# Layer 1's quotients in 32x32 blocks, the ends of its halves behind all its scores, and another order of VectorE's work in the last chunk

## The chip, the cores and the metric

The kernel runs on one core of one Trainium2 chip. The metric is the device time of one execution in microseconds (us), as a median of several runs. A profiled execution gives a trace of every instruction on the engines: TensorE (PE; its weight loads are PEld), VectorE (DVE), ScalarE (ACT), GpSimd (POOL) and SyncE (SP, which here only issues DMAs). Lines such as L1163 are lines of the kernel's file.

## What is computed

Four self-attention layers, one after the other, on x of shape (4, 64, 64, 64): four samples of 4096 positions with 64 channels. The layers differ in the normalisation ahead of them and in the residual; what matters here is layer 1, a SAGAN block whose keys and values are max-pooled to 1024 positions:

```python
theta = x @ w_theta            # 4096 positions x 8
phi   = maxpool2(x @ w_phi)    # 1024 positions x 8
g     = maxpool2(x @ w_g)      # 1024 positions x 32
beta  = softmax(theta @ phi^T) # 4096 x 1024, rows sum to one
out   = x + sigma * ((beta @ g) @ w_o + b_o)
```

(w_theta, w_phi, w_g, w_o are spectrally normalised first.) The other three layers are attention over 4096 x 4096 positions with 64 channels. In all of them the kernel forms exp(scores) without a maximum, multiplies it with the values, and divides by the row sums afterwards: that quotient is what the change is about.

## The kernel before, in words

**The foreground.** `fast_path` (L598) takes the samples s0 to s3 through the layers. Layers 0, 2 and 3 run as attention phases of 64 calls of `step()` (L813) each; with three phases for each of four samples that makes 768 steps. A step issues, in this order: scores for two units (L1290 in layers 2 and 3, L997 in layer 0), 16 matmul records of 512 columns; their exponentials on ScalarE (L1295, L1007), 128x1024 each, from a PSUM score tile into an SBUF tile; then the two accumulations that fall due in this step (exp(scores) times values into PSUM, L1325 or L1028, 16 records). In layers 2 and 3 VectorE adds each exponential tile to a running sum `zacc` (L1301), in pairs. At the end of each chunk of 512 positions, `turn_blocks` and `sum_blocks` transpose zacc in blocks of 32x32 (L1309) and reduce it over 32 (L1313), `sums` (L1239) adds up the partial sums with four small matmuls (L1244, 16 columns each) and takes the reciprocal of 128x16 sums on VectorE (L1249, L1252), and `turn` (L1259) transposes the output's 32x32 blocks (L1264), multiplies by the reciprocals (L1257, L1271) and goes on.

**The background.** Everything else is cut into pieces by `yield` in generators; `background(tempo, ...)` (L779) sets the generator that runs next to a phase, and each step advances it at most once at each of four places: MID (between the step's two accumulations), LATE (inside the second one), END, and ALONE (as MID, but then nothing is done LATE in the same step). The budget is a credit that grows by `tempo` with each step. Work that has a due time of its own goes into the lists `urgent`, `before`, `due` and `later`; `urgent` takes the MID place ahead of the background. The order on every engine is the order in which the program issues (L623, `manual_schedule`); each engine works its queue in that order.

**Buffers.** PSUM holds two score tiles of 128x1024 (`s_tile`, pool of 2) and four accumulators of 128x512 (`acc_tile`, pool of 4). A score tile can only be written again when its reader has finished: ScalarE's exponential, as a rule, or VectorE where a piece has borrowed the tile. SBUF has 13 tiles of `x_tile` and 14 of `p_tile`; `small` and `o_tile` have two of each name.

**Layer 1** (L1063) is background work. For s0 it runs beside layer 0 of s1 (`on` "DVE", `bank` False); for s1, s2 and s3 beside layer 2 of the sample before (`on` "ACT", `bank` True). After its projections (L1076, L1093, L1105) come two halves j of 2048 positions, each with 8 blocks of keys k: `scores(j, k)` (L1121, operands of 8 rows), their exponentials on ScalarE (L1127), their sum on VectorE (`zaccs[j]`, L1136), and `add(j, k)` (L1147) with values of 32 columns, into one accumulator (bank) or into a score tile that VectorE adds up (not bank, L1156); at the end ScalarE moves the accumulator to SBUF (L1158).

Then `finish(j)` for each half: `normalise(j)` and `last(j)`. `normalise` multiplies a matrix of ones with `zaccs[j]`, four calls over 512 columns (L1163), which puts the sums of a position into all 32 rows of its quarter; ScalarE copies that to SBUF and records a sum for the range check (L1169); VectorE takes the reciprocal in four parts of 128x128 (L1172) and multiplies the half's output with it (L1174); ScalarE reads the reciprocals once more for the check (L1176). `last` multiplies with w_o (L1182) and VectorE adds bias and residual (L1184). With `bank`, `finish(0)` begins as soon as half 0 is complete, a piece of it after each block of half 1 (L1212 to L1222), and `finish(1)` follows half 1. Without `bank`, both begin behind all scores and run side by side.

**The last chunk.** In layer 3 of s3, the last chunk's `final` (L1548) replaces `turn`: it works in two parts of 256 columns. `count_bad` (L1826) reduces the range checks to one number by way of a small matmul (L1829), `set_bad` writes it out (L1830), and `read_flag` makes every engine load it before the last stores (L1540): whether a general path runs depends on that number; it does not run here. `most_in_range` (L1813) has checked all earlier sums some steps before.

Of the kernel before, what the change touches and what calls it, by code (L numbers as in the profile page):

```python
# [8 lines left out]
FP = mybir.dt.float32  # L9
I32 = mybir.dt.int32  # L10
AF = mybir.ActivationFunctionType
ALU = mybir.AluOpType
AX = mybir.AxisListType
# [584 lines left out]
def fast_path(tc: tile.TileContext, a: dict, out: bass.AP, bad, read_flag):  # L598
# [9 lines left out]
    nc = tc.nc  # L608
    x = a["x"]
    B, H, W, C = x.shape  # L610
    N = H * W
    P = 128
    W2 = W // 2
    S = N // 2
    NC = S // 512
    NB = N // P
# [3 lines left out]
    MID, ALONE, LATE, END = range(4)  # L620
# [4 lines left out]
    const, small = pool("const", 1), pool("small", 2)  # L625
# [3 lines left out]
    s_tile = lambda: ps_s.tile([P, 1024], FP, tag="s", name="s")  # L629
    acc_tile = lambda: ps_a.tile([P, 512], FP, tag="a", name="acc")  # L630
    x_tile = lambda name: x_p.tile([P, S], FP, tag="x", name=name)
    p_tile = lambda: p_p.tile([P, 1024], FP, tag="p", name="p")
    o_tile = lambda name: o_p.tile([P, 512], FP, tag=name, name=name)
    half = lambda i: slice(i * C, (i + 1) * C)
    quarter = lambda q: slice(q * 32, q * 32 + 32)
    chunk = lambda c: ds(c * 512, 512)
# [18 lines left out]
    def ctile(shape, name):  # L655
        return const.tile(shape, FP, tag=name, name=name)
# [53 lines left out]
    ident = ctile([P, P], "ident")  # L710
    make_identity(nc, ident)
    ones = ctile([P, P], "ones")
    nc.gpsimd.memset(ones, 1.0)
    lanes = ctile([P, C], "lanes")
    nc.vector.tensor_reduce(lanes[:, 0:32], ident.rearrange("p (a j) -> p j a", j=32), AX.X, ALU.add)
    nc.vector.tensor_copy(lanes[:, 32:C], lanes[:, 0:32])

    def twice(dst, src):
        for i in range(2):
# [22 lines left out]
    blocks = {n: (ctile([P, P], f"A{n}"), ctile([P, 1], f"Ab{n}")) for n in (0, 3)}  # L742
# [3 lines left out]
    rows(gamma0, a["L0_conv_gamma"])  # L746


    NCHECK = B * (NB + 2 + 2 * NC * 16)
    all_z, all_r = ctile([P, NCHECK], "all_z"), ctile([P, NCHECK], "all_r")  # L750
    checks = [0]

    def check_columns(n):
        i = checks[0]
        checks[0] += n
        return all_z[:, i : i + n], all_r[:, i : i + n]
# [306 lines left out]
    def layer1(on, st, bank):  # L1063
# [7 lines left out]
        s = s_tile()  # L1071
        for j in range(2):
            for e in range(2):
                for i in range(2):
                    q = 2 * e + (i ^ j)
                    nc.tensor.matmul(  # L1076
                        s[quarter(q), chunk(i)], wth1[half(i), quarter(q)], x1[half(i), chunk(2 * j + e)],
                        start=True, stop=True,
# [3 lines left out]
        NK = M // P  # L1082
# [5 lines left out]
        for j in range(NC // 2):  # L1088
            yield MID
            s = s_tile()  # L1090
# [12 lines left out]
        s = s_tile()  # L1103
# [7 lines left out]
        ps, accs, zaccs, os = {}, {}, {}, {}  # L1111
# [46 lines left out]
                nc.scalar.copy(os[j], acc)  # L1158

        def normalise(j):  # L1160
            z = acc_tile() if bank else s_tile()[:, 0:512]
            for q in range(4):
                nc.tensor.matmul(  # L1163
                    z[quarter(q), :], ones[:, 0:32], zaccs[j][:, q // 2, chunk(q % 2)], start=True, stop=True
                )
            del zaccs[j]
            r = o_tile("r")
            z_column, r_column = check_columns(1)
            nc.scalar.activation(r, z, AF.Copy, accum_out=z_column)  # L1169
            for i in range(4):  # L1170
                yield MID
                nc.vector.reciprocal(r[:, ds(i * P, P)], r[:, ds(i * P, P)])  # L1172
            yield MID
            nc.vector.tensor_tensor(os[j], os[j], r, ALU.mult)  # L1174
            yield MID
            nc.scalar.activation(r, r, AF.Copy, accum_out=r_column)  # L1176

        def last(j):
            s = s_tile()
# [4 lines left out]
            nc.vector.scalar_tensor_tensor(x1[:, wide(j)], s, bo1, x1[:, wide(j)], ALU.add, ALU.add)  # L1184

        def finish(j):

            if not bank:
                yield ALONE
            yield from normalise(j)  # L1190
            yield MID
            yield ALONE
            last(j)

        end = None
        todo = [(j, k) for j in range(2) for k in range(NK)]
        for n in range(len(todo) + 1):
            accumulate = None
            if n < len(todo):
                yield LATE  # L1200
                accumulate = scores(*todo[n])
            if n:
                if not bank:
                    yield END
                elif n == len(todo):
                    yield LATE
                add(*todo[n - 1])
            if accumulate and bank:
                later.append(accumulate)
            elif accumulate:  # L1210
                accumulate()
            if n == NK and bank:  # L1212
                end = finish(0)
                at = next(end)
            elif end is not None:
                yield at
                at = next(end, None)
                end = end if at is not None else None
        while end is not None:
            yield at  # L1220
            at = next(end, None)
            end = end if at is not None else None  # L1222
        if bank:
            yield from finish(1)
        else:
            ends = [finish(j) for j in range(2)]
            at = [next(end) for end in ends]
            while at[0] is not None:
                if at[0] == ALONE:
                    yield ALONE  # L1230
                    at[0] = next(ends[0], None)
                yield at[1]
                at = [at[0] if at[0] != at[1] else next(ends[0], None), next(ends[1], None)]
# [5 lines left out]
    def sums(zsums):  # L1239

        s = s_tile()
        for k in range(2):
            for i in range(2):
                nc.tensor.matmul(  # L1244
                    s[half(i), ds(k * 512, 16)], lanes[half(k), :], zsums[half(k), i * 16 : i * 16 + 16],
                    start=True, stop=True,
                )
        z_columns, r_columns = check_columns(16)
        nc.vector.tensor_reduce(  # L1249
            z_columns, s.rearrange("p (k b) -> p b k", k=2)[:, 0:16, :], AX.X, ALU.add  # L1250
        )
        nc.vector.reciprocal(r_columns, z_columns)  # L1252
        return z_columns, r_columns
# [270 lines left out]
    def layer3(st, not_before):  # L1524


        h = st.pop("x"), st["k"][1]
        dst = out[st["b"]].rearrange("(j e b) (i w) (q f) -> j e b i w q f", e=2, b=16, i=2, q=2)

        def residual(c):  # L1530

            t = o_tile("residual")
            for e in range(2):
                nc.vector.transpose(t[half(e), :], h[0 if e == c % 2 else 1][half(e), chunk(c // 2 * 2 + e)])
            return t

        def store(c, t, rows, queues):
            for n in range(4):
                e, q = divmod(n, 2)
                queues[n % len(queues)](  # L1540
                    dst[c // 2, e, rows, c % 2, :, q, :].rearrange("b w f -> w b f"), blocked(t[quarter(n), :])[:, rows, :]
                )

        def last(c, t):
            nc.vector.tensor_tensor(t, t, residual(c), ALU.add)
            store(c, t, slice(0, 16), [nc.sync.dma_start])

        def final(acc, zsums):  # L1548

            z_columns, r_columns = sums(zsums)  # L1550
            rest_in_range(z_columns, r_columns)
            t = o_tile("turned")
            parts = [slice(m * 256, m * 256 + 256) for m in range(2)]
            for m, cols in enumerate(parts):
                o = o_tile("o")[:, 0:256]
                nc.scalar.copy(o, acc[0][:, cols])
                nc.vector.tensor_tensor(o, o, acc[1][:, cols], ALU.add)
                nc.vector.transpose(t[:, cols], o)
                if m == 0:
                    set_bad = count_bad()  # L1560
            for m, cols in enumerate(parts):
                divide(blocked(t[:, cols]), t[:, cols], r_columns[:, m * 8 : m * 8 + 8])
                if m == 0:
                    set_bad()
                nc.vector.tensor_tensor(t[:, cols], t[:, cols], kept[0][:, cols], ALU.add)
            flag.append(read_flag())
            for m in range(2):
                store(NC - 1, t, slice(m * 8, m * 8 + 8), [nc.sync.dma_start, nc.scalar.dma_start])

        kept = []  # L1570
        ends = st["b"] == B - 1
        if ends:
            before.setdefault(now[0] + NC * NB // 2 - 8, []).append(lambda: later.append(lambda: kept.append(residual(NC - 1))))
        return attention(st, last, not_before, "done3", final if ends else None)
# [14 lines left out]
    t = s_tile()[:, 0:P]  # L1589
# [5 lines left out]
    t = s_tile()[:, 0:1]  # L1595
# [65 lines left out]
    at = 10 * C  # L1661
    loaded = {}
    for n, dsts in spectra:
        w_d, u_d = a["L1_conv_w_" + n], a["L1_conv_u_" + n]
        r, d = w_d.shape
# [147 lines left out]
    def most_in_range():  # L1813
        assert checks[0] == NCHECK - count
        for i, (seen, bound) in enumerate(((all_z, SUM_MAX), (all_r, 1.0 / SUM_MIN))):
            seen = seen[:, 0 : NCHECK - count]
            nc.vector.tensor_scalar(seen, seen, bound, None, ALU.is_le)
# [71 lines left out]
```

## Time and profile before

| what | value |
|---|---|
| three runs, median (lowest to highest) | 2941.55 us (2941.31 to 2942.19) |
| the profiled execution, its own time | 2942.68 us |
| its span on the trace, from first to last instruction | 2940.5 us |
| granted TensorE clock, mean | 0.999 of full speed |
| busy: ScalarE, VectorE, GpSimd | 65%, 63%, 1% |
| a plain step (16 score and 16 accumulation records) | 3.43 us |
| the same with the score and value matmuls of one block of layer 1 (bank) | 5.64 us |

A step's length is read off the trace as the distance between the first score matmuls of one step and of the next. "Span" is what the trace covers; the profiled execution's own time is 2.2 us longer. In the lists of groups a line gives the operation, output and input, partitions x columns, the number of instructions, their busy time and the mean of one in nanoseconds; then the idle time of the engine ahead of them and what ended it. The chain of waits follows the work back from the last instruction, each time to what released it.

### The profile page before, as it was taken

What the parts mean: (1) busy time and instruction counts of PE and PEld (TensorE: products, weight loads), DVE (VectorE), ACT (ScalarE), POOL (GpSimd) and SP (SyncE); (2) the same over time, 40 slices, a digit from 0 to 9 for tenths busy, and PEclk for the clock granted to TensorE, in tenths of its full rate; (3) what the DMA queues carried; (4) which work ended last, traced back from release to release, by engine and by line L of the source; (5) the groups of instructions that cost most, each with busy time, mean ns of one, the idle gap of its engine ahead of it and who ended that gap; (6) DMA issues with size and microseconds to landing.
All of it is one profiled execution on the core that took longest, in us unless ns stands there. A gap on an engine that the chain in (4) does not pass through costs nothing.

```text
span 2940.5 us, 66599 instructions
## 1 busy us (share of the span) xinstructions
PE 2910.9 (99%) x29349; PEld 1169.8 (40%) x29349; DVE 1846.6 (63%) x2112; ACT 1923.4 (65%) x2769; POOL 33.6 (1%) x32
## 2 busy tenths in 40 slices
PE   9999999999999999999999999999999999999998
PEld 3333235333544433444443334444344444443332
DVE  1211742588831068872017888888988877878877
ACT  6877778666588866567886665655655555655554
POOL 0000000000000000000000000000000000000000
PEclk9999999999999999999999999999999999999999
DMA  2010000000002000000000000000000100000000
GB/s 38 1 30 5 1 2 7 13 5 12 13 5 30 1 5 5 19 6 13 6 1 5 5 21 7 20 5 9 5 19 5 23 5 7 6 19 5 8 5 10
DMA packets 76778, 30.12 MB, mean 10 GB/s; under 512 B 70464, under 2 KB 74560, under 8 KB 75072
## 3 DMA queue, kind: packets, MB, share of 16 engines
q1 hardware_dynamic: 74224, 25.37, 4.6%
q8 instruction: 232, 3.80, 0.5%
q10 hardware_dynamic: 2256, 0.41, 0.1%
q14 instruction: 66, 0.54, 0.1%
HBM read 4.79 MB, written 4.19 MB: 3 GB/s over the span
## 4 chain that ended last, share of the span: by engine, by line
PE 97%; DVE 1%; ACT 1%; SPq 0%; issue 0%; DMA 0%; ACTq 0%; DVEq 0%
PE acc L1325 30%; PE s L1290 30%; PE acc L1028 15%; PE s L997 15%; PE s L1121 2%; PE acc L1147 2%; ACT p L1127 1%; PE s L1147 1%; DVE zacc L1301 0%; PE s L888 0%; PE s L909 0%; PE s L1421 0%; PE s L1093 0%; PE s L1182 0%; PE s L1469 0%
## 5 line engine op out<-in xcount | busy, mean ns | idle before, releaser
L1295 ACT ACTIVATE p<-s 128x1024 f32<-128x1024 f32 x1024 | 993.7, 1022 | 687.7 <-PE s L1290 654.9
L1301 DVE TENSOR_TENSOR zacc<-zacc,p 128x1024 f32<-128x1024 f32 x960 | 1173.2, 1222 | 182.6 <-ACT p L1295 119.3
L1325 PE MATMUL acc<-p,v 64*64 64x512 f32 (+1 forms) x8576 | 1019.9, 572 | 0.0
L1325 PEld LDWEIGHTS acc<-p,v 64*64 64x64 f32 x8576 | 356.4, 133 | 532.9 <-issue 529.2
L1028 PE MATMUL acc<-p,vs 64*64 64x512 f32 (+1 forms) x4224 | 513.5, 578 | 0.5 <-ACT vs L1017 0.5
L1007 ACT ACTIVATE p<-s 128x1024 f32<-128x1024 f32 x480 | 486.9, 1015 | 32.9 <-PE s L997 14.0
L1290 PE MATMUL s<-q,k 64*64 64x512 f32 x2048 | 498.0, 590 | 1.7 <-ACT p L1127 1.7
L997 PE MATMUL s<-xT,q 64*64 64x512 f32 x2048 | 488.8, 591 | 2.6 <-DVE mean L1357 0.7
L1290 PE MATMUL s<-q,xT 64*64 64x512 f32 x2048 | 490.2, 589 | 0.0
L997 PE MATMUL s<-xT,q_swapped 64*64 64x512 f32 x2048 | 489.1, 591 | 0.7 <-DVE o L1156 0.7
L1290 PE MATMUL s<-q,h_swapped 64*64 64x512 f32 x2048 | 479.3, 589 | 0.2 <-DVE v L1446 0.2
L1290 PE MATMUL s<-q,k_swapped 64*64 64x512 f32 x2048 | 476.2, 590 | 0.0
L1009 DVE TENSOR_REDUCE all_z<-z 128x1 f32<-128x4 f32 x128 | 20.1, 157 | 624.4 <-ACT p L1007 624.1
L1028 PEld LDWEIGHTS acc<-p,vs 64*64 64x64 f32 x4224 | 186.7, 133 | 262.4 <-issue 199.0
L1017 ACT ACTIVATE vs<-v,all_r 64x64 f32<-64x64 f32 x512 | 176.7, 345 | 139.5 <-PE acc L1028 70.8
L997 PEld LDWEIGHTS s<-xT,q_swapped 64*64 64x64 f32 x2048 | 149.7, 133 | 143.3 <-issue 108.8
L1290 PEld LDWEIGHTS s<-q,h_swapped 64*64 64x64 f32 x2048 | 150.1, 133 | 135.4 <-issue 127.5
L1290 PEld LDWEIGHTS s<-q,xT 64*64 64x64 f32 x2048 | 150.5, 133 | 133.2 <-issue 127.4
L1290 PEld LDWEIGHTS s<-q,k_swapped 64*64 64x64 f32 x2048 | 149.9, 133 | 132.8 <-issue 88.3
L997 PEld LDWEIGHTS s<-xT,q 64*64 64x64 f32 x2048 | 149.3, 133 | 127.4 <-issue 96.7
L1290 PEld LDWEIGHTS s<-q,k 64*64 64x64 f32 x2048 | 150.2, 133 | 112.7 <-issue 94.2
L1127 ACT ACTIVATE p<-s 128x1024 f32<-128x1024 f32 x128 | 124.1, 1021 | 80.7 <-PE s L1121 80.7
(218 smaller groups left out, 1320.8 us busy)
## 6 DMA issues: line engine op xcount, KB each, us to landing
k_swapped<-k SPq DMA_DIRECT2D x8, 512.0 KB, 5.4
residual<-turned SPq DMA_DIRECT2D x128, 32.0 KB, 1.8
h_swapped<-xT SPq DMA_DIRECT2D x8, 512.0 KB, 5.8
out_dram<-turned SPq DMA_DIRECT2D x60, 64.0 KB, 2.0
xin<-in_x_dram SPq DMA_DIRECT2D x12, 256.0 KB, 6.3
q_swapped<-q SPq DMA_DIRECT2D x6, 512.0 KB, 5.7
pg<-pg SPq DMA_DIRECT2D x8, 128.0 KB, 2.3
xin<-in_x_dram SPq DMA_DIRECT2D x12, 64.0 KB, 2.4
```

The source lines that it names most:

```text
L997: nc.tensor.matmul(s[half(e), chunk(i)], queries(m, i, e), k[half(i), chunk(c)], start=True, stop=True)
L1007: nc.scalar.activation(p, s, AF.Exp, accum_out=z)
L1009: nc.vector.tensor_reduce(zsum[:, m : m + 1], zs.pop(m), AX.X, ALU.add)
L1017: nc.scalar.activation(vs[half(e), :], v[half(e), m, :], AF.Copy, scale=rz[half(e), m : m + 1])
L1028: nc.tensor.matmul(acc[c][half(i), cols], vs[half(e), :], ps[2 * t + n][half(e), chunk(i)][:, cols], start=(m == 0 and e == 0), stop=(m == ...
L1121: nc.tensor.matmul(ss[e][half(m), chunk(i)], pgs[0 if e == d else 1][r, ds(n * P + m * C, C)], th[r, chunk(i ^ j)], start=True, stop=True,)
L1127: nc.scalar.activation(pk[e], ss[e], AF.Exp)
L1147: nc.tensor.matmul(acc[quarter(q), :], g[:, k, :], ps[j, k][q // 2][:, chunk(q % 2)], start=(k == 0 or not bank), stop=(k == NK - 1 or not ...
L1290: nc.tensor.matmul(s[half(e), chunk(i)], k[(j + i) % 2][half(i), ds(j // 2 * P + e * C, C)], q[half(i), chunk(c)], start=True, stop=True,)
L1295: nc.scalar.activation(p, s, AF.Exp)
L1301: add = lambda: nc.vector.tensor_tensor(zaccs[c], p0, p, ALU.add)
L1325: nc.tensor.matmul(accs[c][e][half(i), cols], v[half(e), j, :], p[half(e), chunk(i)][:, cols], start=(j == 0), stop=(j == NB - 1),)
```

## The change

Three edits.

1. `normalise` no longer multiplies by ones. It transposes the two parts of `zaccs[j]` in 32x32 blocks on VectorE and reduces each over 32 (as `turn_blocks` and `sum_blocks` do), eight small matmuls of 16 columns bring the partial sums together in a borrowed score tile (in two rounds that add up), VectorE adds them, takes the reciprocal of 128x16, transposes the half's output, multiplies, and transposes it back. ScalarE has no part in it. The constant `lanes` becomes wider (a memset on GpSimd and three reduces on VectorE instead of a reduce and a copy), since the four positions of a quarter need it shifted. The range check takes 16 columns for each half in place of one, 1280 in all instead of 1160.
2. With `bank`, `finish(0)` and `finish(1)` both run behind all scores of both halves, one after the other.
3. In `final`, both of ScalarE's copies are issued first, and VectorE does the first part's division and residual ahead of the second part's addition and transpose.

```diff
--- before.py
+++ after.py
@@ -711,9 +711,12 @@
     make_identity(nc, ident)
     ones = ctile([P, P], "ones")
     nc.gpsimd.memset(ones, 1.0)
-    lanes = ctile([P, C], "lanes")
-    nc.vector.tensor_reduce(lanes[:, 0:32], ident.rearrange("p (a j) -> p j a", j=32), AX.X, ALU.add)
-    nc.vector.tensor_copy(lanes[:, 32:C], lanes[:, 0:32])
+
+    lanes = ctile([P, 5 * 32], "lanes")
+    nc.gpsimd.memset(lanes, 0.0)
+    for i in (0, 1, 3):
+        nc.vector.tensor_reduce(lanes[:, i * 32 : i * 32 + 32], ident.rearrange("p (a j) -> p j a", j=32), AX.X, ALU.add)
+    both_lanes, lanes_of = lanes[:, 0:C], (lanes[:, 3 * 32 : 5 * 32], lanes[:, 2 * 32 : 4 * 32])
 
     def twice(dst, src):
         for i in range(2):
@@ -746,7 +749,7 @@
     rows(gamma0, a["L0_conv_gamma"])
 
 
-    NCHECK = B * (NB + 2 + 2 * NC * 16)
+    NCHECK = B * (NB + 2 * 16 + 2 * NC * 16)
     all_z, all_r = ctile([P, NCHECK], "all_z"), ctile([P, NCHECK], "all_r")
     checks = [0]
 
@@ -1158,22 +1161,33 @@
                 nc.scalar.copy(os[j], acc)
 
         def normalise(j):
-            z = acc_tile() if bank else s_tile()[:, 0:512]
-            for q in range(4):
-                nc.tensor.matmul(
-                    z[quarter(q), :], ones[:, 0:32], zaccs[j][:, q // 2, chunk(q % 2)], start=True, stop=True
-                )
+
+            zsums = small.tile([P, 4 * 16], FP, tag="zsums1", name="zsums1")
+            for e in range(2):
+                yield MID
+                t = p_tile()
+                nc.vector.transpose(t, zaccs[j][:, e, :])
+                yield MID
+                nc.vector.tensor_reduce(zsums[:, ds(e * 32, 32)], t.rearrange("p (n k) -> p n k", k=32), AX.X, ALU.add)
             del zaccs[j]
-            r = o_tile("r")
-            z_column, r_column = check_columns(1)
-            nc.scalar.activation(r, z, AF.Copy, accum_out=z_column)
-            for i in range(4):
-                yield MID
-                nc.vector.reciprocal(r[:, ds(i * P, P)], r[:, ds(i * P, P)])
-            yield MID
-            nc.vector.tensor_tensor(os[j], os[j], r, ALU.mult)
-            yield MID
-            nc.scalar.activation(r, r, AF.Copy, accum_out=r_column)
+            yield MID
+            s = s_tile()
+            for i in range(2):
+                for k in range(2):
+                    for e in range(2):
+                        nc.tensor.matmul(
+                            s[half(e), ds(k * 512, 16)], lanes_of[i][half(k), :], zsums[half(k), ds((2 * e + i) * 16, 16)],
+                            start=(i == 0), stop=(i == 1),
+                        )
+            z_columns, r_columns = check_columns(16)
+            nc.vector.tensor_reduce(z_columns, s.rearrange("p (k b) -> p b k", k=2)[:, 0:16, :], AX.X, ALU.add)
+            nc.vector.reciprocal(r_columns, z_columns)
+            t = o_tile("r")
+            nc.vector.transpose(t, os[j])
+            yield MID
+            blocks = t.rearrange("p (b f) -> p b f", f=32)
+            nc.vector.tensor_tensor(blocks, blocks, r_columns.unsqueeze(2).to_broadcast([P, 16, 32]), ALU.mult)
+            nc.vector.transpose(os[j], t)
 
         def last(j):
             s = s_tile()
@@ -1184,15 +1198,11 @@
             nc.vector.scalar_tensor_tensor(x1[:, wide(j)], s, bo1, x1[:, wide(j)], ALU.add, ALU.add)
 
         def finish(j):
-
-            if not bank:
-                yield ALONE
             yield from normalise(j)
             yield MID
             yield ALONE
             last(j)
 
-        end = None
         todo = [(j, k) for j in range(2) for k in range(NK)]
         for n in range(len(todo) + 1):
             accumulate = None
@@ -1209,19 +1219,9 @@
                 later.append(accumulate)
             elif accumulate:
                 accumulate()
-            if n == NK and bank:
-                end = finish(0)
-                at = next(end)
-            elif end is not None:
-                yield at
-                at = next(end, None)
-                end = end if at is not None else None
-        while end is not None:
-            yield at
-            at = next(end, None)
-            end = end if at is not None else None
         if bank:
-            yield from finish(1)
+            for j in range(2):
+                yield from finish(j)
         else:
             ends = [finish(j) for j in range(2)]
             at = [next(end) for end in ends]
@@ -1242,7 +1242,7 @@
         for k in range(2):
             for i in range(2):
                 nc.tensor.matmul(
-                    s[half(i), ds(k * 512, 16)], lanes[half(k), :], zsums[half(k), i * 16 : i * 16 + 16],
+                    s[half(i), ds(k * 512, 16)], both_lanes[half(k), :], zsums[half(k), i * 16 : i * 16 + 16],
                     start=True, stop=True,
                 )
         z_columns, r_columns = check_columns(16)
@@ -1551,14 +1551,14 @@
             rest_in_range(z_columns, r_columns)
             t = o_tile("turned")
             parts = [slice(m * 256, m * 256 + 256) for m in range(2)]
-            for m, cols in enumerate(parts):
-                o = o_tile("o")[:, 0:256]
+            os = [o_tile("o")[:, 0:256] for _ in parts]
+            for o, cols in zip(os, parts):
                 nc.scalar.copy(o, acc[0][:, cols])
+            for m, (o, cols) in enumerate(zip(os, parts)):
                 nc.vector.tensor_tensor(o, o, acc[1][:, cols], ALU.add)
                 nc.vector.transpose(t[:, cols], o)
                 if m == 0:
                     set_bad = count_bad()
-            for m, cols in enumerate(parts):
                 divide(blocked(t[:, cols]), t[:, cols], r_columns[:, m * 8 : m * 8 + 8])
                 if m == 0:
                     set_bad()
```

## Prediction

> **What bounds the kernel now.** I read the page's engine line first, then its chain, then the groups, then chain and timelines around each place that the diff touches.
>
> ```profile
> PE 2910.9 (99%) x29349; PEld 1169.8 (40%) x29349; DVE 1846.6 (63%) x2112; ACT 1923.4 (65%) x2769; POOL 33.6 (1%) x32
> PE 97%; DVE 1%; ACT 1%; SPq 0%; issue 0%; DMA 0%; ACTq 0%; DVEq 0%
> ```
>
> TensorE is busy 99% of the span and holds 97% of the chain that ended last. So the time is TensorE's records, plus the few places where it waits; time of VectorE or ScalarE counts only where it makes TensorE wait.
>
> The chain around the end of layer 1's half 1 (first of the three bank samples; the three are alike); columns: start, length, what:
>
> ```profile
> 676.61 0.86 PE acc L1325 x8
> 677.47 0.86 PE s L1182 x8
> 678.33 0.99 PE acc L1163 x8
> 679.32 1.02 PE acc L1325 x8
> 680.34 1.72 PE s L1290 x16
> 682.06 1.72 PE acc L1325 x16
> ...
> 702.66 0.85 PE acc L1325 x8
> 703.51 0.08 PE s L1244 x7
> 703.59 0.90 PE acc L1325 x8
> ```
>
> A plain step is 1.72 + 1.72 = 3.43 us. Eight records of 512 columns cost 0.86, in L1182 as in L1325. L1163 and the L1325 behind it hold 0.99 + 1.02 = 2.01 where two groups should hold 1.72: alone among 64x64 tiles L1163 costs 0.86 + 0.30 = 1.16. The four small matmuls of L1244 cost 3.55 - 3.43 = 0.12 in their step.
>
> The chain at the end of half 0, then ScalarE's timeline there:
>
> ```profile
> 619.70 1.04 PE s L1121 x16
> 620.74 1.00 PE acc L1147 x8
> 621.74 0.86 PE acc L1163 x8
> 622.60 1.88 PE s L1290 x16
> 624.48 1.29 PE acc L1325 x16
> 625.76 1.65 PE s L1121 x16
> ```
>
> ```profile
> 622.64 0.59 ACT L1158 COPY o<-acc 128x512 f32<-128x512 f32 x1
> 623.11 0.63 ACT L1169 ACTIVATE r<-acc 128x512 f32<-128x512 f32 x1
> 623.86 0.57 ACT L1334 COPY o<-acc 128x512 f32<-128x512 f32 x1
> 624.32 1.94 ACT L1295 ACTIVATE p<-s 128x1024 f32<-128x1024 f32 x2
> ```
>
> L1163 stands next to L1147, which has its tile shape, and costs a bare 0.86. But L1121 takes 1.65 for 1.04 one step later: three ScalarE copies stand ahead of the exponentials that free the score tiles. That step is 6.30 for 5.64.
>
> The groups concerned, and the end of the last chunk:
>
> ```profile
> L1309 DVE STREAM_TRANSPOSE p<-zacc 128x1024 f32<-128x1024 f32 x32 | 39.9, 1245 | 2.7
> L1313 DVE TENSOR_REDUCE zsums<-p 128x32 f32<-128x1024 f32 x32 | 38.8, 1211 | 0.7
> L1172 DVE RECIPROCAL r<-r 128x128 f32<-128x128 f32 x32 | 29.5, 935 | 0.0
> ```
>
> ```profile
> 2931.74 0.14 DVE L1830 TENSOR_SCALAR bad<-acc 1x1 int32<-1x1 f32 x1
> 2931.85 0.43 DVE L1565 TENSOR_TENSOR turned<-turned,residual 128x256 f32<-128x256 f32 x1
> 2932.49 3.50 SPq L1540 DMA_DIRECT2D out_dram<-turned  x4
> ```
>
> **What the Trainium skill says.** "TensorEngine Tiling (Array Packing)", Key Properties: changing the tiling mode drains TensorE. The trace agrees: 1.16 for a lone L1163, 0.86 beside its like. The same page, Instruction Overhead: a matmul has a fixed cost of about 60 cycles, so below that width the columns don't matter. That fits L1244, paid by count. "VectorE: DVE Perf Modes", First, the fixed hardware budget: the reciprocal is an iterative divide with repeat count 8; the trace has 935 ns for 128 columns. "TensorE: Matmul & The Clock Gate", Architectural detail: VectorE and ScalarE take their queues strictly in order. The copies ahead of the exponentials above show it; so what the change queues on VectorE delays what stands behind.
>
> **The change, part by part.** The sum is against the profiled execution (2942.68; span 2940.5, 2.2 around it; it lies 1.1 above the median), in TensorE time.
>
> *Half 0 of a bank sample.* Its L1163 goes: 0.86 in the step at 616.09 (6.44 us). Not all of it is gained: L1121's exponentials only end at 622.76 (620.82 + 1.94), so the next step's scores, now 0.86 earlier, would wait some 0.23: -0.63. One step later L1169 (0.63 + 0.20, from 623.11 to the next start 0.75) no longer stands ahead of the exponentials, but L1158 and L1334 still do; of the 0.66 excess I let 0.54 stand: -0.12. Total -0.75. Bounds: -0.5 (bubble twice as long, no relief) to -1.46 (0.80 and all of the 0.66).
>
> *Half 1 of a bank sample.* The step at 674.71 holds L1182 of half 0 and a lone L1163: 5.45 = 3.43 + 0.86 + 1.16. L1182 is only moved (two of 0.86 before and after, each alone in a step, all 64x64); L1163 goes: -1.16. The bound is close, since one view shows all of it.
>
> *The small matmuls.* Eight calls, 16 records, in two rounds, each like L1244's: 2 x 0.12 = 0.24 per half, in the middle of a step among 64x64 tiles. The second round adds onto the first, which no row shows; bounds 0.12 (hidden like the weight loads) and 0.50.
>
> A bank sample: -0.75 - 1.16 + 2 x 0.24 = -1.43; three: -4.29.
>
> *The sample without bank.* Two steps of 1.16 in L1163 go: 2 x 1.16 = 2.32. (The step with the first also has 0.96 of waiting for VectorE's L1156; that stays, behind another piece.) Both halves' small matmuls now come in one step: 0.48, and the second takes the score tile of that step's second exponential, so it waits 0 to 1.0; I take 0.3. Together -1.54, bounds -0.8 to -2.1.
>
> *VectorE's queue.* Per half, before: 4 x 0.94 + 0.68 = 4.4 us. After: 2 x 1.25 + 2 x 1.21 + 0.19 + 0.25 + 3 x 0.67 = 7.4. I cost it at nothing, and this is what hides it. A pair of L1301 takes 2.41 of a step's 3.43. With a transpose (1.17 to the next issue) it is 3.58, with a reduce (1.08) 3.49: VectorE falls behind by 0.15 and 0.06, 0.42 over four steps, and by up to about 2 with the chunk's own ending, before a plain step gives back 1.0. Queued behind are the reader of the small matmuls' score tile and L1184's add behind L1182. A late reader costs TensorE only what goes beyond the 1.72 of accumulation between two scores. Following the new order, the adds keep 0.2 to 0.4 in hand, the small readers about 1.7. If that cover is gone, each microsecond of lag costs up to one per add, six times.
>
> *ScalarE* loses L1169 and L1176, 0.8 each per half: nothing beyond the relief counted. *Start:* two more reduces (0.37 each) for a copy (0.24) are some 0.5 on VectorE, which waits for TensorE 1.9 later in any case; the memset (0.2) likewise: 0. *Range check:* 120 more columns near the end, some 0.4 of VectorE, under about 1.0 free per step in the six steps left: 0. *Other pieces:* the background behind layer 1 starts earlier or later by a few steps; one step now has a 0.28 stall at its L909: 0 to -0.28, taken 0.
>
> *The last chunk.* VectorE has the same instructions in another order, so its end stays within 0.1. The first half's sum is done earlier: o, transpose, least (to 2930.70), division (to 2931.0), then the flag (matmul's answer there by 2930.95) at 2931.0 for 2931.74, the addition ends near 2931.5 for 2932.28. Flag load and first stores come 0.74 earlier; the last pair only as far as it hangs on the queue: the third store's issue takes 2.09 us and ends at 2935.50, the span at 2940.5. If that queue sets the end, -0.74; if the last addition (to 2933.07), 0. I take -0.7, bounds 0 and -1.0.
>
> Sum: -4.29 - 1.54 - 0.7 = -6.5. Profiled 2936.2; against the median 2941.55: **2935.0**.
>
> **The rivals.** *Larger:* half 0's stall goes wholly (-1.46 each, 2.1 more), second rounds are hidden (eight by 0.12, 1.0 more), L909 and tail at their best (0.6 more): -10.2, 2931.4. For it: that stall is ScalarE's alone. Against: two of three copies stay.
>
> *Smaller:* the second round waits for the first (0.50 per half in six, 1.6 less), the group without bank waits 1.0 (0.7 less), the tail hangs on the last addition (0.7 less): -3.5, 2938.0. For it: each is a wait that the trace of before cannot show.
>
> *Slower:* VectorE's lag holds the score tiles. Place: L1182's add and the small readers, six each. If each comes behind one more pair (2.41), an add costs 2.41 - 0.3 = 2.1 and a small reader 2.41 - 1.7 = 0.7: 6 x 2.8 = 16.8, less 6.5 is +10.3: 2951.8. It decides from 6.5 / 6 + 0.3 = 1.4 us of extra lag at each add. For it: steps over 3.43 on VectorE at 63% load overall, and over 80% in most later slices of the page. Against: they are four in a row, and plain steps follow. One 128x1024 instruction of extra lag (1.22) would leave -6.5 + 5.5 = -1.0: 2940.5.
>
> That the change doesn't do what it says is excluded by its instruction order: L1163 and L1172 are gone, and steps are 768 as before.
>
> **How the numbers follow.** Likeliest 0.50, larger 0.16, smaller 0.26, slower 0.08. Range: the larger case's end to one instruction of lag, 2931.4 to 2940.5, leaving out the slower case and the far ends. A measurement of this kernel can tell about 0.2%, 5.9 us, from no change, so the bound is 2935.7, just above my time. Of the likeliest case (-6.5, give or take 1.5) 0.34 lies below it: faster 0.16 + 0.34 = 0.50, same 0.16 + 0.26 = 0.42, slower 0.08.
>
> **What would show it.** Right: the step of 5.45 becomes 3.43 and two steps of 4.29 exist for the two L1182; steps with the small matmuls are 3.67; the 6.44 step is near 5.8; first L1540 at 0.7 less from the end of TensorE's work. Wrong: idle time ahead of L1290 or L1121 put down to VectorE's small reduce or to L1182's add; steps with the small matmuls over 4.0; a last store issue no earlier than before.

## The result, and the profile after

| | before | after |
|---|---|---|
| median of 15 runs (lowest to highest) | 2941.97 us (2940.23 to 2942.34) | 2935.14 us (2934.01 to 2936.14) |
| the profiled execution, its own time | 2942.68 us | 2934.01 us |
| its span | 2940.5 us | 2932.3 us |

The ratio is 0.9977, with a 95% interval of 0.9969 to 0.9985: 6.8 us less. The interval leaves out 1, and reaches to both sides of the 0.2% that the prediction drew as its line. The prediction was 2935.0.

The page's line of engines, after:

```profile
PE 2901.1 (99%) x29413; PEld 1129.5 (39%) x29413; DVE 1870.4 (64%) x2145; ACT 1913.8 (65%) x2737; POOL 33.7 (1%) x33
```

TensorE has 64 records more than before and 9.8 us less of busy time: 64 wide records of L1163 went, 128 narrow ones of L1178 came. VectorE works 24 us more and it doesn't show in the time. The groups behind both (count, busy us, mean ns):

```profile
L1169 DVE STREAM_TRANSPOSE p<-zacc 128x1024 f32<-128x1024 f32 x16 | 19.6, 1233 | 0.0
L1171 DVE TENSOR_REDUCE zsums<-p 128x32 f32<-128x1024 f32 x16 | 19.2, 1210 | 0.0
...
L1178 PE MATMUL s<-zsums,lanes 64*64 64x16 f32 x128 | 3.1, 200 | 0.5 <-ACT p L1010 0.5
```

The chain at the end of half 1 in the first bank sample, after. Line numbers of layer 1 are 3 to 14 higher than before: L1124 is the old L1121, L1150 the old L1147, L1161 the old L1158, L1196 and L1198 the old L1182 and L1184.

```profile
671.12 1.72 PE s L1290 x16
672.84 1.72 PE acc L1325 x16
...
686.57 0.85 PE acc L1325 x8
687.43 0.20 PE s L1178 x15
687.62 0.90 PE acc L1325 x8
...
700.66 0.86 PE acc L1325 x8
701.51 0.86 PE s L1196 x8
702.37 0.86 PE acc L1325 x8
```

Where a step of 5.45 us stood (at 674.71 before), there is now a plain one of 3.43 (at 670.94). The small matmuls of a half make a step of 3.67, and the product with w_o (L1196) stands in a step of its own of 4.29.

The end of half 0, the same sample: the chain, then ScalarE's timeline.

```profile
616.62 1.09 PE s L1124 x16
617.72 0.02 issue
617.74 1.03 ACT p L1130
618.77 0.04 issue
618.82 2.00 PE s L1290 x16
620.82 1.29 PE acc L1325 x16
622.11 1.54 PE s L1124 x16
```

```profile
617.74 1.94 ACT L1130 ACTIVATE p<-s 128x1024 f32<-128x1024 f32 x2 [1.68 <-PE s L1124]
619.56 0.59 ACT L1161 COPY o<-acc 128x512 f32<-128x512 f32 x1
620.03 0.62 ACT L1334 COPY o<-acc 128x512 f32<-128x512 f32 x1
620.50 1.99 ACT L1295 ACTIVATE p<-s 128x1024 f32<-128x1024 f32 x2
```

With L1163 gone, TensorE waits for the exponential L1130, as forecast: the step is 5.81 for 6.44. (The 1.1 us of the chain on ScalarE are not all waiting; L1150 runs on TensorE beside them.) Two copies still stand ahead of the next exponentials, so L1124 still takes 1.54 for 1.04, and that step is 6.24 for 6.30.

The last chunk, lines that answer to those of before:

```profile
2924.41 0.15 DVE L1830 TENSOR_SCALAR bad<-acc 1x1 int32<-1x1 f32 x1
2924.49 0.43 DVE L1565 TENSOR_TENSOR turned<-turned,residual 128x256 f32<-128x256 f32 x1
2924.83 0.41 DVE L1558 TENSOR_TENSOR o<-o,acc 128x256 f32<-128x256 f32 x1
2925.18 3.45 SPq L1540 DMA_DIRECT2D out_dram<-turned  x4
```

Counted from the start of the last copy L1556 on ScalarE, the first store goes out after 2.91 us for 3.64.

Laid step against step, before and after, the difference is this:

| place | us |
|---|---|
| up to the end of the first four steps | -1.52 |
| sample without bank | -1.20 |
| the three bank samples (-1.57, -1.86, -0.51) | -3.94 |
| other steps, together | +0.08 |
| from the last step to the end | -1.66 |
| span | -8.24 |

The first four steps, which wait for the loads, look like chance: with the old constant one other profile had them 0.75 us shorter than the kernel before, with the new constant another had them 0.3 longer (both below). That is why the profiles differ by more than the medians.

### The profile page after: what moved, and what is told of

Read it like the earlier page. It is cut to its first block, busy times and chain, and to the rows that moved or that the text cites. A ratio compares the mean times of both kernels' runs of the same rounds, so it can differ in the third digit from the quotient of the medians.

```text
span 2932.3 us, 66740 instructions
## 1 busy us (share of the span) xinstructions
PE 2901.1 (99%) x29413; PEld 1129.5 (39%) x29413; DVE 1870.4 (64%) x2145; ACT 1913.8 (65%) x2737; POOL 33.7 (1%) x33
## 4 chain that ended last, share of the span: by engine, by line
PE 84%; DVE 1%; ACT 0%; issue 0%; DVEq 0%; ACTq 0%
PE acc L1325 30%; PE s L1290 30%; PE acc L1031 10%; PE s L1000 9%; PE s L1124 2%; PE acc L1150 2%; DVE zacc L1301 1%; PE s L1421 0%; PE s L891 0%; PE s L912 0%; PE s L1469 0%; PE s L1196 0%; ACT p L1130 0%; PE s L1096 0%; PE s L1441 0%
## 5 line engine op out<-in xcount | busy, mean ns | idle before, releaser
L1301 DVE TENSOR_TENSOR zacc<-zacc,p 128x1024 f32<-128x1024 f32 x960 | 1174.0, 1223 | 178.1 <-ACT p L1295 112.7
L1325 PEld LDWEIGHTS acc<-p,v 64*64 64x64 f32 x8576 | 342.3, 133 | 540.3 <-issue 540.3
L1010 ACT ACTIVATE p<-s 128x1024 f32<-128x1024 f32 x480 | 487.0, 1015 | 34.7 <-PE s L1000 16.0
L1290 PE MATMUL s<-q,k 64*64 64x512 f32 x2048 | 491.1, 590 | 2.1 <-ACT p L1130 2.1
L1031 PEld LDWEIGHTS acc<-p,vs 64*64 64x64 f32 x4224 | 180.4, 133 | 267.0 <-issue 202.0
L1130 ACT ACTIVATE p<-s 128x1024 f32<-128x1024 f32 x128 | 124.1, 1021 | 82.3 <-PE s L1124 82.3
```

Source lines behind the costliest of these rows:

```text
L1010: nc.scalar.activation(p, s, AF.Exp, accum_out=z)
L1031: nc.tensor.matmul(acc[c][half(i), cols], vs[half(e), :], ps[2 * t + n][half(e), chunk(i)][:, cols], start=(m == 0 and e == 0), stop=(m == ...
L1130: nc.scalar.activation(pk[e], ss[e], AF.Exp)
L1290: nc.tensor.matmul(s[half(e), chunk(i)], k[(j + i) % 2][half(i), ds(j // 2 * P + e * C, C)], q[half(i), chunk(c)], start=True, stop=True,)
L1301: add = lambda: nc.vector.tensor_tensor(zaccs[c], p0, p, ALU.add)
L1325: nc.tensor.matmul(accs[c][e][half(i), cols], v[half(e), j, :], p[half(e), chunk(i)][:, cols], start=(j == 0), stop=(j == NB - 1),)
```

## The experiments

Line numbers in their profiles are those of each kernel. All times are beside runs of the kernel before on the same chip (medians of 2941.4 to 2941.7 us).

**The quotients alone (e1_blocks).** The changed `normalise`, with the old order of ends and the old last chunk:

```diff
+            if n == NK and bank:
+                end = finish(0)
+                at = next(end)
+            elif end is not None:
+                yield at
...
         if bank:
-            for j in range(2):
-                yield from finish(j)
+            yield from finish(1)
```

> The quotients in 32x32 blocks alone: with bank, half 0's end is again interleaved with half 1's scores, and the last chunk is as before. Theory (TensorE's records are the gain, the move of the ends gives nothing): the steps of 6.44, 6.30 and 5.45 us become 5.81, 6.24 and 4.29, each half's small matmuls cost 0.24, so a bank sample gains 1.4 and the sample without bank 1.2 as after; about 2936.9, 1.7 above the changed kernel, of which 0.7 is the last chunk. Rival (the move is needed, because VectorE, which in half 1's steps has a pair of L1301 and a pair of the half's own sum, 4.9 of 5.64 us, falls behind with a transpose or reduce on top): the step with half 0's small matmuls is over 6.5 us and others of half 1 over 5.9; 2939 or more.

2942.57 us, ratio 1.0004 (0.9995 to 1.0013): no gain. The theory fell. The expected gains are all there (5.81 for 6.44, 4.29 for 5.45, the sample without bank 1.2 less), and they are given back: in each bank sample two steps of half 1 take 6.51 and 6.00 for 5.64, and later ones 3.93, 4.15 and 3.61 for 3.43. Less 0.24 for the small matmuls that is 2.3 to 2.4 us a sample, 7.1 in three. VectorE's timeline ahead of the first of these steps (L1312 is the foreground's pair, L1139 the half's own, L1169 the new transpose, L1486 the reader of a score tile in layer 2's last projection, L1475 before):

```profile
642.38 2.35 DVE L1139 TENSOR_TENSOR zacc<-zacc,p 128x1024 f32<-128x1024 f32 x2
644.65 1.24 DVE L1169 STREAM_TRANSPOSE p<-zacc 128x1024 f32<-128x1024 f32 x1
645.81 2.51 DVE L1312 TENSOR_TENSOR zacc<-zacc,p 128x1024 f32<-128x1024 f32 x2
648.24 2.35 DVE L1139 TENSOR_TENSOR zacc<-zacc,p 128x1024 f32<-128x1024 f32 x2
650.51 1.27 DVE L1486 SCALAR_TENSOR_TENSOR xT<-s,bp,xT 128x256 f32<-128x256 f32 x2
```

and TensorE's scores (L1301 here) in that step:

```profile
650.68 0.60 PE L1301 MATMUL s<-q,k_swapped 64*64 64x512 f32 x2
651.92 0.65 PE L1301 MATMUL s<-q,k_swapped 64*64 64x512 f32 x2 [0.65 <-DVE xT L1486]
```

VectorE has no gap anywhere in this stretch: two pairs, 4.9 us, and 1.2 of quotient work against a step of 5.64. What stands behind comes late, and its score tile with it. So far the rival was right, with its mechanism: 32x32 blocks cost VectorE more than half 1's steps have free. (The step over 6.5 us is not that of the small matmuls, as the rival had it, but the one behind layer 2's projection.)

That is only 1.0 of the 2.4 us. The other 1.4 are lost behind half 1, in steps that have one pair of additions, as in the changed kernel. There half 1's quotients meet the end of layer 2's chunk (its transpose L1320, its reduce L1324) in VectorE's queue. The chain, first sample:

```profile
691.26 1.25 DVE p L1320
692.50 1.10 DVE zsums L1171
693.60 1.13 DVE zsums L1324
...
703.56 0.11 DVE all_z L1260
```

From 690.00 to 703.67 it stays on VectorE, until L1260, the reader of the chunk's own small matmuls, frees a score tile; TensorE's next scores start at 703.72. VectorE had stood idle for 2.44 us shortly before (ahead of L1198, at 676.70, waiting for the product with w_o), with half 1's quotients queued behind that.

**The move alone (e2_ends).** The old `normalise`, with both ends behind all scores:

```diff
-            if n == NK and bank:
-                end = finish(0)
...
         if bank:
-            yield from finish(1)
+            for j in range(2):
+                yield from finish(j)
```

> The ends of both halves behind all scores alone, with the old quotients by a matrix of ones. Theory (moving gives nothing by itself): half 0's L1163 stands beside L1147 again, in another step, at 0.86; the steps of 6.44 and 6.30 become 5.81 and 6.24 since ScalarE's copy of the sums is gone from there, and the 0.86 comes back where L1163 now stands: +0.2 for each of three samples, about 2942.5. Rival (half of the gain is ScalarE's relief that the move brings): 2940 or less.

2942.44 us, ratio 1.0003 (0.9994 to 1.0012). The steps are as the theory had them: 5.81 for 6.44, 6.24 for 6.30, and 5.45 for 4.59 where half 0's L1163 now stands beside L1147 (0.86). Half 1's, away from its like and in one step with the product with w_o, costs 2.02 with it, 0.86 and 1.16. One step of the third sample was new: L1244's, 4.32 for 3.55. It appears in the changed kernel too (4.34) and not in e1_blocks, so it belongs to the move: the ends now run later, layer 2's background pieces with them, and there L1501 on ScalarE comes between L1244 and the exponential that frees its score tile. So neither edit gains alone, and both together do. The moved ends lie in steps of 3.43 us in which VectorE has one pair of 2.41, not two; and half 0's transposes and reduces are done (at 684.0 us in the first sample) when the chunk's end begins (L1309 at 686.9), while half 1's come behind it. No run has both edits without the third. What they gain together is read from the steps: 5.1 us by the table above, where e1_blocks, counted in the same way, loses 1.0.

**The last chunk alone (e3_tail).** Both copies first, the first part's division ahead of the second part's addition, as in the change.

> Only the order of VectorE's work in the last chunk. Theory (the third store waits on the queue, which moves with the first stores): first stores 0.74 us earlier counted from the last small matmuls, the end with them: 2941.2. Rival 1 (the last addition sets the end): no change, 2942.0. Rival 2 (the 1.6 us by which the changed kernel's stretch from the last step to the end was shorter is all of this edit): 2940.4.

2940.74 us for 2941.44, ratio 0.9998 (0.9989 to 1.0007): the interval can't tell. The profiles can. From the start of L1556's last copy to the end, four kernels with the old order took 10.96 to 11.67 us, five with the new one 9.66 to 10.01: 1.4 less in the mean, with no overlap. The first store goes out 0.74 earlier in all five, the last issue 0.9 earlier in the mean (5.4 to 5.9 for 6.2 to 6.7).

**The constant alone (e4_lanes).** The memset, the three reduces and the slices, in the kernel before.

> Only the wider constant (a memset on GpSimd, three reduces on VectorE for a reduce and a copy); nothing else uses the new columns. Theory (the first steps were 1.5 us shorter in the changed kernel's profile by chance of when the loads landed): 2942.0, and the first four steps differ from the kernel before by no fixed amount. Rival (the order at the start moved something for good): first steps 1.5 us shorter here too, 2940.5.

2941.82 us, ratio 1.0000 (0.9991 to 1.0009); the first four steps 0.3 us longer than before. In e2_ends, which has the old constant, the first scores came at 9.8 us for 13.0, as in the changed kernel (9.7), and the four steps ended 0.75 earlier. The constant doesn't decide it, so the theory of chance stands.

**The small matmuls apart (e5_apart).** In the changed kernel:

```diff
-            yield MID
+            yield MID if bank else ALONE
             s = s_tile()
             for i in range(2):
```

> The changed kernel with one edit: in the sample without bank the two halves' small matmuls come in two steps in place of one (their piece is ALONE there). Theory (the step of 4.54 us holds 0.48 of matmuls and 0.63 of waiting for the second score tile, whose reader is that step's second exponential): two steps of 3.67 in place of 4.54 and 3.43, so 0.63 less than the changed kernel, 2934.5. Rival (the second round's adding onto the first costs that): the two steps sum to the same 1.1 over plain, 2935.1.

Two steps of 3.67 in place of 4.54 and 3.43: 0.64 less, as the theory had it. The median is 2935.17 us (ratio 0.9979, 0.9970 to 0.9988), level with the changed kernel: 0.6 us is less than the runs can tell. In the changed kernel's timeline one sees the wait: 0.45 us of idle time shown (ends of records are modelled; by the steps' lengths it is 0.63), for ScalarE's exponential L1010:

```profile
407.58 0.37 PE L1178 MATMUL s<-zsums,lanes 64*64 64x16 f32 x16
408.41 0.42 PE L1178 MATMUL s<-zsums,lanes 64*64 64x16 f32 x16 [0.45 <-ACT p L1010]
408.66 1.07 PE L1031 MATMUL acc<-p,vs 64*64 64x512 f32 x8
```

**A longer queue on VectorE (e6_lag).** In the changed kernel:

```diff
         def last(j):
+            spare = p_tile()
+            for _ in range(2):
+                nc.vector.transpose(spare, x1[:, wide(j)])
             s = s_tile()
```

> The changed kernel with two needless 128x1024 transposes on VectorE (1.17 us each to the next issue) right ahead of L1196's add, at each of its eight places; their result is not used. It prices the slower rival of the prediction. Theory (the add keeps 0.2 to 0.4 us in hand, all beyond makes the next scores wait): each of the six steps with bank behind L1196 2.0 us longer, 12 us in all, 2947. Rival (more in hand than the walk through the queue gave, a microsecond or more): 8 us or less, 2943 or less.

2953.20 us, ratio 1.0040 (1.0025 to 1.0056): 18 more than the changed kernel. Behind the six adds with bank it is 14.2, for the theory's 12. Half 0's adds cost 2.5, 2.5 and 4.2 us, half 1's 1.5, 1.9 and 1.5; the sample without bank, which the theory left out, paid 4.2 once. The chain at half 0's add in the second sample (L1195 are the needless transposes, L1201 the add, L1293 and L1328 scores and accumulation):

```profile
1212.21 1.25 DVE p L1195
...
1213.56 1.30 DVE xT L1201
1214.86 0.04 issue
1214.90 1.09 PE s L1293 x8
1215.99 1.72 PE acc L1328 x16
```

The needless pair moves the end of half 0's adds by 2.6 us. By the steps' lengths these had 0.1 us of that in hand, by TensorE's idle time ahead of the scores (2.29) 0.3. Half 1's adds end only 1.6 to 1.9 later, since VectorE had a gap ahead of them (0.9 us in the first sample), and their steps lose about as much: the rest is covered by the gap. The six adds sum to more than 12 mainly because of one place with 1.7 us that isn't waiting, told at the end; the sample without bank has another.

**Half 0's copy on VectorE (e7_copy).** e5_apart, and:

```diff
-                nc.scalar.copy(os[j], acc)
+                (nc.vector.tensor_copy if bank and j == 0 else nc.scalar.copy)(os[j], acc)
```

> The changed kernel with the small matmuls apart as in the run e5_apart, and with half 0's copy out of PSUM on VectorE in place of ScalarE (bank only). Theory (in the step of 6.24 us, 0.60 over its like, L1161's and L1334's copies stand ahead of the exponentials; without L1161 some 0.5 of it goes, three times): 1.5 us less than with the small matmuls apart alone, 2933.0. Rival (VectorE's copy comes late behind its pairs, and the accumulator is then missed by the next chunk): no gain, 2934.5 or more.

2933.59 us, ratio 0.9974 (0.9964 to 0.9984): 1.6 less than e5_apart. The step of 6.24 is 5.75 in all three samples. ScalarE's timeline there:

```profile
618.79 1.94 ACT L1130 ACTIVATE p<-s 128x1024 f32<-128x1024 f32 x2 [1.68 <-PE s L1124]
620.62 0.59 ACT L1334 COPY o<-acc 128x512 f32<-128x512 f32 x1
621.08 1.98 ACT L1295 ACTIVATE p<-s 128x1024 f32<-128x1024 f32 x2
```

It is the fastest kernel here. It lies clear below the kernel before; against the changed kernel there are only the two medians, which differ by 1.6.

**The second part's stores later (e8_late, e9_late).** In the kernel before:

```diff
             for m, cols in enumerate(parts):
+                if m == 1:
+                    for _ in range(2):
+                        nc.vector.transpose(o_tile("o")[:, 0:256], t[:, cols])
                 divide(blocked(t[:, cols]), t[:, cols], r_columns[:, m * 8 : m * 8 + 8])
```

> The kernel before, with two needless 128x256 transposes (0.37 us each to the next issue) on VectorE ahead of the second part's division in the last chunk: the second part's stores can go out 0.75 us later, the first part's as before. Counted from the last ScalarE copy (L1556), five profiles with the new order end after 9.66 to 10.01 us, four with the old one after 10.96 to 11.67. Theory A (the second part's stores wait on the queue behind the first part's, and that sets the end): the last issue stays between 6.2 and 6.7 and the end between 10.9 and 11.7. Theory B (the last addition sets the end): both 0.75 later, the end at 11.7 or more. Theory C (stores that crowd each other land late, and spacing them helps): the end before 10.9.

> The same kernel once more, for a second profile of its end: as for e8_late.

e8_late 2941.43 us, ratio 0.9999 (0.9989 to 1.0009); e9_late 2942.05 us in one run. The ends are 11.18 and 11.20 us after the last copy, within the old range and below the 11.7 of theory B. But the second part's stores, 0.5 later at 5.05, were held for less at their first issues (0.3 to 0.4 us for 0.8 to 2.1), and the last issue came earlier, at 5.5. Theory A asked for 6.2 to 6.7 there, so it isn't confirmed. C, whose end was to be below 10.9, can't be dismissed either: at the program's end (L1888) the last DRAIN of every other queue starts at 2939.0 us or before, VectorE's at 2939.6 and 2939.9. So in these two profiles VectorE's queue, the one with the added work, holds the end by some 0.6 to 0.9 us; without that it would come at 10.6 and 10.3, an estimate from these figures. The two runs don't settle what sets the end in the others.

## Why the prediction was right, and where not

*Half 0 with bank*, -0.75 forecast: -0.69. The first step's gain, 0.86 less the bubble behind the exponential, was met to the hundredth (0.63); the relief of ScalarE was 0.06 for 0.12. Of the 0.60 that stays in the second step, e7_copy puts 0.49 down to one of the two other copies, L1161. By its own terms the bound for a bubble twice as long is -0.4, not -0.5 (0.86 less 0.46).

*Half 1 with bank*, -1.16 forecast: 2.02 less in one step and 0.86 paid in another, -1.16. That the lone L1163 carried 0.30 more than its records is borne out, in e2_ends too. That it is the change of tile shape which costs this is argued from the two places of L1163; no run varied the shape alone.

*Small matmuls*, 0.24 a half: 0.23 and 0.24. The second round costs what the first does.

*The sample without bank*, -1.54 forecast: -1.20. The term that was off is the wait for the second score tile, taken as 0.3 in a range of 0 to 1.0; it is 0.63, and e5_apart takes it away.

*VectorE's queue at nothing*: right for the changed kernel's layer 1, with two steps of 0.1 and one of 0.05. (Much later, at 2604.95, a step is 0.36 longer, waiting for VectorE's L916; e5_apart and e7_copy have it, e6_lag doesn't, and its cause is open.) e6_lag measured the cover that the prediction named, 0.2 to 0.4 us in hand at the adds: 0.1 to 0.3 at half 0's, and a gap of VectorE's on top at half 1's. And e1_blocks shows the slower rival at work, in the same queue but in other places: among half 1's scores, and where half 1's quotients meet the chunk's end. The prediction costed the move of the ends only by its records; that without it the whole gain is lost, it didn't say. Its argument against that rival ("plain steps follow") was not enough by itself: in e1_blocks the larger part of the loss falls in plain steps.

*Other pieces*, 0 to -0.28: the stall at L909 went (-0.28), and so did 0.5 in two steps of the second sample, but one L1244 step of the third sample took 0.8 more. The prediction had looked for no loss there; e2_ends puts it down to the move.

*The last chunk*, -0.7 with bounds 0 and -1.0: mis-sized. The first stores came 0.74 earlier as worked out, but the stretch to the end is 1.4 shorter in the mean of the profiles, beyond the bound. The last issue is 0.9 earlier, so the 0.74 are passed on and 0.2 more. The rest doesn't lie in the stores' landing: in all eleven profiles their last transfer is over 2.4 to 3.7 us ahead of the program's end. It shows on ScalarE's queue, behind its branch on the range check (L1850). Before, that branch is at 2936.1 us and the queue's next instruction at 2939.6; after, at 2928.7 and 2931.4. This stretch is 3.0 to 3.6 us in the four profiles with the old order and 2.7 to 2.9 in the five with the new one, 0.6 less in the mean. What ScalarE waits for there stays open.

*The start and the range check* at nothing: e4_lanes agrees for the start; no step near the end changed.

The errors were small and of both signs: without bank 0.3 less gain, the third sample 0.8 less, two stalls of 0.3 and 0.5 gone that were counted at nothing, the last chunk 0.7 more. That is why the change, forecast as 6.5, came out as 6.8; the time itself came within 0.2 us because the kernel before also measured 0.4 above the median that was used. Agreement to that digit is luck.

## What to carry to other kernels

Where one engine is busy 99%, a change is priced by laying steps side by side and counting that engine's records, with a lone change of tile shape as a cost of its own. Work that is moved off that engine has to be placed where the engine that takes it has time free, and clear of what that engine does at the same moment for others: here the same blocks lost 1 us in one place, among steps with two pairs of additions and on top of a chunk's end, and gained 5 in another. Before spending a hidden engine's slack, measure it by putting needless work into its queue.

## What the runs showed of the hardware that was not expected

After two of its waits TensorE came back at half its clock. In e6_lag, behind the first bank add (2.29 us of idle time) and behind the add in the sample without bank (2.27), its busy time and clock by stretch (columns: stretch, length, busy and records, clock, DMA share, GB/s):

```profile
705.00:709.00 4.00, 4.00 (x44) 1.00 0.14 34
712.34:715.75 3.41, 3.41 (x20) 0.50 0.02 4
716.40:718.00 1.60, 1.60 (x20) 1.00 0.00 0
425.62:429.03 3.41, 3.41 (x20) 0.50 0.00 0
```

In the first place, the 8 records of scores and 16 of accumulation that came next took 1.81 + 2.69 = 4.5 us, for 1.09 + 1.72 = 2.8 behind the same wait of 2.29 us in the second and third sample. In the sample without bank the next 16 took 3.64 us, where behind a wait without a slower clock 1.09 + 0.86 = 1.95 would do. So a stall on the bounding engine can cost up to 1.7 us more than itself.

The Trainium skill, "TensorE: Matmul & The Clock Gate", What's actually happening, has the clock fall after an idle window of about 3.4 us that runs free of the kernel. The traces agree on the window: in each of the eleven, all changes of the granted clock lie whole multiples of 3.413 us apart (in e6_lag 121, 1, 83, 1 and 653 of them). They differ on how idle it must be. Laid out on this grid, every window at full clock in which TensorE was idle for 1.90 us or more by its records (13 in all, 11 of them at the end of the program) was followed by half the clock, and none with 1.57 us or less was. That also tells the four waits of 2.3 us in e6_lag apart: the two with a slower clock lie wholly in one window, the other two are cut by a boundary into 1.5 + 0.8 and 1.6 + 0.7. This is read from the traces; no run varied the idle time, and between 1.57 and 1.90 us nothing was seen.
